# Two 1x1 maps made once, in column halves of the TensorE array, and copied three times by ScalarE

## The chip, the cores and the metric

The kernel runs on one core of one Trainium2 chip. The metric is the device time of one execution in microseconds (us). A core has a matrix engine (TensorE, PE in the profile, with its weight loads shown apart as PEld), a vector engine (VectorE, DVE), an engine for activations (ScalarE, ACT), a general engine (GpSimd, POOL) and one that here only issues transfers (SyncE, SP). Each of them works through its own instructions in order; they wait for one another by semaphores. TensorE's results land in PSUM, a small memory which DVE and ACT read; everything else lies in SBUF.

## The reference, cut to what matters

Input `x` has 8 images of 256 channels and 64x64 pixels, float32. Two layers follow each other: a block with weights made from the data (layer 0), and a block with local attention and a dynamic convolution (layer 1). Each begins with a group norm and ends with a residual sum. The change lies in the beginning of layer 0:

```python
x1 = _conv1x1(x, w1, b1)                 # 256 -> 32 channels
x2 = _conv1x1(x, w2, b2)                 # 256 -> 32 channels
x3 = _conv1x1(x, w3, b3)                 # 256 -> 256 channels
x2p = jnp.pad(x2, ((0, 0), (0, 0), (1, 1), (1, 1)), mode='reflect')
x2u = _unfold3(x2p).reshape(B, REL * K * K, H, W)   # the 9 neighbours of each pixel
h = jnp.concatenate([x1, x2u], axis=1)
h = jax.nn.relu(_bn(h, ...)); h = _conv1x1(h, cw1)
h = jax.nn.relu(_bn(h, ...)); w = _conv1x1(h, cw2, cb2)   # 9 weights per pixel and group
out = jnp.einsum('bgskhw,bgkhw->bgshw', x3u, w)     # x3u: the 9 neighbours of x3
```

So `x2` is needed at nine shifts, of which three are shifts of the column by -1, 0 and +1.

## The kernel before, in words

An image is cut into 8 bands of 8 rows, 512 pixels, so there are 64 bands. All matmuls are float32. One matmul of the program appears as two MATMUL records and two LDWEIGHTS records in the trace: the four records of `p12` in a band are two matmuls, one for each half of the 256 input channels.

**The maps (`small_maps`, L319 to L348).** For a band, TensorE makes one PSUM tile `p12` of 128 partitions by 512 pixels (L325; the trace calls it `p`). The stationary weights `w12s` hold `w2` three times and `w1` once, side by side: 32 + 32 + 32 + 32 columns. So three quarters of the output partitions carry the same map x2. ScalarE adds the bias and writes the four quarters to the SBUF tile `x2`, partitions to the same partitions: x2 shifted by one column (L332), unshifted (L332), shifted the other way (L332), and x1 (L335). Two more small activations fill the reflected border column of the two shifted copies, 8 values a partition, again from PSUM (L337, L338). Then GpSimd copies border rows from and to the neighbouring bands' tiles (L343, or L345 and L346; L348).

**What follows.** `hidden_maps` (L397) turns `x2` into `hid` on ScalarE (L406) and multiplies it on TensorE into `ph`, in four column groups of 32 (L417). `tap_weights` (L429) makes nine weights per pixel (L435), VectorE multiplies them with the neighbours of x3 (L448), GpSimd adds the products up in `xg` (L456). `value_maps` (L350) makes x3 (L357, L362).

**Scaled weights (`scaled_weights`, L288 to L317).** Once per image the group norm's scale is multiplied into `w12` and `w3` by VectorE (L296, L297), and its shift goes through the weights to the biases, by narrow matmuls (L304) and small additions (L311, L313).

**The order of the work** is written out by hand. The main loop runs over `g` from -12 to 63; for each g it makes 8 steps `s` (L971, L973). Layer 1 works on band g, layer 0 twelve bands ahead: the maps of band g + 12 are made in step 0 of g. For g below 0 only layer 0 runs (`alone`). Within a step, parts of the work are placed at fixed points by two lists, `mid` and `end`, and by `after(n, ...)`:

```python
if 0 <= g + AHEAD < B * NB:
    bq_, iq = divmod(g + AHEAD, NB)
    if s == 0:
        mid.append(lambda: small_maps(bq_, iq))
    if s == (2 if alone else 0):
        (mid if alone else end).append(lambda: value_maps(bq_, iq, 0))
```

In step 0 of a usual g, TensorE's order around the maps is: first half of the dynamic weights `pf` (L814), a transposed value tile (L595), the maps (L325), the weighted values (L736, 64-column halves of the array), second half of `pf` (L814), x3 (L357), and then the scores of step 1 (L692) and the transposed probabilities (L724). Where band g is the first of an image (i = 0), two value maps (L551) come just ahead of L325 instead of the value tile.

**PSUM tiles** of the tag `gen` are five, taken in turn: `p12` is one of them, and the fifth `gen` tile after it has to wait until ScalarE has read `p12` for the last time. On ScalarE the reads of `p12` stand behind L718 (probabilities), L597 or the value copies L560 to L569, and ahead of L819 (exponentials of `pf`), L362 (x3) and L726 (copy of the transposed probabilities). GpSimd's in-order queue has, around the maps, the sums L1010 and L825, then the border rows L343 to L348, then L842.

Of the kernel before, what the change touches and what calls it, by code (L numbers as in the profile page):

```python
# [10 lines left out]
F32 = mybir.dt.float32  # L11
BF16 = mybir.dt.bfloat16
AF = mybir.ActivationFunctionType
# [5 lines left out]
P = 128  # L19
C = 256  # L20
NCT = C // P
H = W = 64
HW = H * W
R = 8
BAND = R * W
# [5 lines left out]
REL = 32  # L31
# [41 lines left out]
PG, PB, PM, PV, PB21, PG2, PB2, PM2, PV2, PCB2 = 0, 3, 6, 9, 12, 13, 14, 15, 16, 17  # L73
# [13 lines left out]
def conv_layers_kernel(ctx: ExitStack, tc: tile.TileContext, ins: dict, out: bass.AP):  # L87
    nc = tc.nc
# [18 lines left out]
    def load(name, shape, src=None, now=True):  # L107
        t = const.tile(shape, F32, name=f"c_{name}")
        late.append(lambda: nc.scalar.dma_start(out=t, in_=ins[name] if src is None else src))
        if now:  # L110
            late.pop()()
        return t

    gmat = load("gmat", [P, P])
    par = load("par", [P, NPAR])
    chan = load("chan", [P, NCT, NCHAN], ins["chan"].rearrange("(t p) n -> p t n", p=P))
    rowp = load("rowp", [P, NROW], ins["rowp"].partition_broadcast(P))
    w12 = load("w12", [P, NCT, P], ins["w12"].rearrange("(t p) n -> p t n", p=P))
    w3 = load("w3", [P, NCT, C], ins["w3"].rearrange("(t p) n -> p t n", p=P))
    c1 = load("c1", [P, 3, REL])  # L120
    gq = load("gq", [P, P])
# [59 lines left out]
    w0 = ctx.enter_context(tc.tile_pool(name="l0", bufs=2))  # L181
    w1 = ctx.enter_context(tc.tile_pool(name="l1", bufs=2))
    ps = ctx.enter_context(tc.tile_pool(name="ps", bufs=1, space=PSUM))
# [31 lines left out]
    def after(n, f):  # L215
        later.append((place[0] + n, f))
# [71 lines left out]
    def scaled_weights(b):  # L288

        im = images[b]  # L290

        def scale(sc, bi):
            im.w12s = w0.tile([P, NCT, P], F32, tag="w12s", name=f"w12s_{b}", bufs=1)
            im.w3s = w0.tile([P, NCT, C], F32, tag="w3s", name=f"w3s_{b}", bufs=1)
            for kt in range(NCT):
                nc.vector.tensor_scalar(im.w12s[:, kt], w12[:, kt], sc[:, kt : kt + 1], None, ALU.mult)  # L296
                nc.vector.tensor_scalar(im.w3s[:, kt], w3[:, kt], sc[:, kt : kt + 1], None, ALU.mult)  # L297
            after(5, lambda: through(bi))

        def through(bi):  # L300
            pb = ps.tile([P, 1 + NCT], F32, tag="gen", name=f"pb_{b}", bufs=5)
            for m, w in enumerate((w12, w3[:, :, :P], w3[:, :, P:])):
                for kt in range(NCT):
                    nc.tensor.matmul(  # L304
                        pb[:, m : m + 1], w[:, kt], bi[:, kt : kt + 1], start=(kt == 0), stop=(kt == NCT - 1)
                    )
            after(2, lambda: biases(pb))

        def biases(pb):
            im.bias = w0.tile([P, 1 + NCT], F32, tag="bias", name=f"bias_{b}")  # L310
            nc.vector.tensor_add(im.bias[:, 0:1], pb[:, 0:1], par[:, PB21 : PB21 + 1])  # L311
            for ct in range(NCT):
                nc.vector.tensor_add(  # L313
                    im.bias[:, 1 + ct : 2 + ct], pb[:, 1 + ct : 2 + ct], chan[:, ct, CB3 : CB3 + 1]
                )

        gn_affine([im.st0[:, ct] for ct in range(NCT)], gmat, f"a{b}", scale)  # L317

    def small_maps(b, i):  # L319


        im = images[b]
        p12 = ps.tile([P, BAND], F32, tag="gen", name=f"p12_{b}_{i}", bufs=5)
        for kt in range(NCT):
            nc.tensor.matmul(p12, im.w12s[:, kt, :], im.xc[i][:, kt, :], start=(kt == 0), stop=(kt == NCT - 1))  # L325
        p12 = p12.rearrange("p (r c) -> p r c", r=R)
        t = im.x2[i] = w0.tile([P, HR, W], F32, tag="x2", name=f"x2_{b}_{i}", bufs=2)
        bias = im.bias
        for q, (dst, src) in enumerate(((1, 0), (0, 0), (0, 1))):
            n = W - (q != 1)  # L330
            s = slice(32 * q, 32 * q + 32)
            nc.scalar.activation(  # L332
                t[s, 1 : 1 + R, dst : dst + n], p12[s, :, src : src + n], AF.Identity, bias=bias[s, 0:1]
            )
        nc.scalar.activation(t[96:128, 0:R, :], p12[96:128], AF.Identity, bias=bias[96:128, 0:1])  # L335

        nc.scalar.activation(t[0:32, 1 : 1 + R, 0:1], p12[0:32, :, 1:2], AF.Identity, bias=bias[0:32, 0:1])  # L337
        nc.scalar.activation(  # L338
            t[64:96, 1 : 1 + R, W - 1 : W], p12[64:96, :, W - 2 : W - 1], AF.Identity, bias=bias[64:96, 0:1]
        )  # L340

        if i == 0:
            nc.gpsimd.tensor_copy(t[0:96, 0, :], t[0:96, 2, :])  # L343
        else:
            nc.gpsimd.tensor_copy(t[0:96, 0, :], im.x2[i - 1][0:96, R, :])  # L345
            nc.gpsimd.tensor_copy(im.x2[i - 1][0:96, R + 1, :], t[0:96, 1, :])  # L346
        if i == NB - 1:
            nc.gpsimd.tensor_copy(t[0:96, R + 1, :], t[0:96, R - 1, :])  # L348
# [507 lines left out]
    def beside(g, s):  # L856
# [52 lines left out]
# [6 lines that stand above are left out]
            if s == (3 if alone else 1):  # L915
                mid.append(lambda: value_maps(bq_, iq, 1))
# [33 lines left out]
    with tc.manual_schedule():  # L950

        for i, use in enumerate(("xc", "xc", "xr", "xr", "xs", None, None, None)):
            t = None
            if use is None:
                t = w1.tile([P, NCT, RP, W], F32, tag="yp", name=f"x_{i}", bufs=3)
                t = t.rearrange("p t r c -> p t (r c)")[:, :, :BAND]
# [14 lines left out]
        for g in range(-AHEAD, B * NB):  # L971
            b, i = divmod(g, NB)
            for s in range(STEPS):  # L973
                ct, m = divmod(s, NT // 2)
# [55 lines left out]
def _layout(inputs):  # L1030

    a = {k.replace("L0_conv_", "a_").replace("L1_conv_", "b_"): np.asarray(v) for k, v in inputs.items()}
    f = np.float32
    arr = {"x": a["x"].reshape(a["x"].shape[0], C, HW)}
    arr["w12"] = np.concatenate([a["a_w2"].T] * 3 + [a["a_w1"].T], axis=1)
    arr["w3"] = a["a_w3"].T

    def branch(v):

        o = np.zeros((P, 3) + v.shape[1:], f)  # L1040
        u = v[REL:].reshape((REL, 3, 3) + v.shape[1:])
        o[:96] = np.moveaxis(u, 2, 0).reshape((96, 3) + v.shape[1:])
        o[96:, 0] = v[:REL]
        return o

    arr["c1"] = branch(a["a_cw1"].T)

    quarter = np.tile(np.eye(REL, dtype=f) / NQR, (NQR, 1))
    arr["gq"] = np.tile(quarter, (1, NQR))
    arr["gc"] = np.repeat(quarter, SHARE, axis=1).reshape(P, NCT, P)  # L1050
    par = np.zeros((P, NPAR), f)
    for at, n in ((PG, "g"), (PB, "b"), (PM, "m"), (PV, "v")):
        par[:, at : at + 3] = branch(a[f"a_bn1_{n}"])
    par[:, PB21] = np.concatenate([a["a_b2"]] * 3 + [a["a_b1"]])
    for at, n in ((PG2, "g"), (PB2, "b"), (PM2, "m"), (PV2, "v")):
        par[:, at] = np.tile(a[f"a_bn2_{n}"], NQR)
    par[:, PCB2 : PCB2 + KK] = np.tile(a["a_cb2"].reshape(REL, KK), (NQR, 1))
    arr["par"] = par

    c2 = a["a_cw2"].reshape(REL, KK, REL).transpose(2, 1, 0)  # L1060
    arr["c2"] = np.zeros((P, KK, P), f)
    for q in range(NQR):
        arr["c2"][q * REL : (q + 1) * REL, :, q * REL : (q + 1) * REL] = c2

    chan = np.zeros((C, NCHAN), f)
    chan[:, CB3] = a["a_b3"]
    chan[:, CBQ] = a["b_bq"]
    chan[:, CBK] = a["b_bk"]
    chan[:, CBV] = a["b_bv"]
    chan[:, CBP] = np.tile(a["b_bp"], HEADS)  # L1070
    chan[:, CWP0 : CWP0 + 2] = np.tile(a["b_Wp"], (HEADS, 1))
    chan[:, CW1 : CW1 + KK] = a["b_w1"].reshape(C, KK)
    chan[:, CW2 : CW2 + KK] = a["b_w2"].reshape(C, KK)
    arr["chan"] = chan
    arr["wq"], arr["wk"], arr["wv"] = a["b_Wq"].T, a["b_Wk"].T, a["b_Wv"].T

    arr["wfc"] = a["b_Wfc"].reshape(C, KK, C)[:, [0, 1, 2, 3, 5, 6, 7, 8, 4]].transpose(2, 1, 0)

    loc = np.pad(np.linspace(-1.0, 1.0, W, dtype=f), PAD, mode="reflect")
    arr["rowp"] = np.concatenate(  # L1080
        [loc, a["b_rate1"].reshape(1), a["b_rate2"].reshape(1)]
    )

    arr["gmat"] = np.kron(np.eye(P // 8, dtype=f), np.full((8, 8), 0.125, f))
    q, k = np.arange(NQ), np.arange(NKEY)
    dr = k[None] // KW - q[:, None] // TQ
    dc = k[None] % KW - q[:, None] % TQ
    inside = (dr >= 0) & (dr < KA) & (dc >= 0) & (dc < KA)
    arr["mask"] = np.tile(np.where(inside, 0.0, NEG).astype(f), (2, 1))
    return {n: np.ascontiguousarray(v) for n, v in arr.items()}  # L1090
# [19 lines left out]
```

The softmax here doesn't subtract the row's maximum and nothing guards it: scores larger than these inputs give would overflow.

## Time and profile before

| | |
|---|---|
| three timed runs | 4334.35, 4330.35, 4332.86 us, median 4332.86 |
| span of the profiled execution | 4333.4 us |
| TensorE (PE) busy | 4174.8 us, 96% of the span |
| VectorE, ScalarE, GpSimd busy | 83%, 71%, 67% |
| maps of x1 and x2 on TensorE (L325) | 256 records, 124.5 us busy |
| copies of them on ScalarE (L332, L335, L337, L338) | 64 x (3 + 1 + 1 + 1) activations |
| granted TensorE clock | 0.992 of full speed over the span |

A row of the groups reads: line, engine, operation, what it writes and reads, shapes, count; then busy time in us and the mean duration of one in ns; then the idle time of the engine just before them, with what ended it. For TensorE a mean duration includes the way through the array and overlaps the next record; what a record costs is the distance from one start to the next, or busy time divided by count. "128*64" in a TensorE row would be 128 rows and 64 columns of the array, and "128x512" the shape of the moving operand.

### The profile page before, as it was taken

To read this page: it belongs to the slowest core of one execution; us is meant where nothing else is said; L and a number is where in the kernel's file an instruction comes from. 1 tells how busy PE (TensorE), PEld (TensorE's weight loads), DVE (VectorE), ACT (ScalarE), POOL (GpSimd) and SP (SyncE) were. 2 spreads that over 40 slices of the span, in tenths; PEclk is the share of its full clock that TensorE was granted. 3 is DMA by queue.
4 is the path that set the end of the run, shared out by engine and by line. 5 is a ranking of instruction groups with operands and counts; after the bars stand their busy time and mean duration, and the time that the engine had idled before them with its cause. 6 is when DMAs were issued, how large, how long until landed. Compare 5 with 4: busy or idle time off the path is not lost.

```text
span 4333.4 us, 72039 instructions
## 1 busy us (share of the span) xinstructions
PE 4174.8 (96%) x25004; PEld 2104.1 (49%) x25004; DVE 3577.6 (83%) x7244; ACT 3059.9 (71%) x7598; POOL 2900.3 (67%) x1778
## 2 busy tenths in 40 slices
PE   6789999999999999999999999999999999999998
PEld 3344445444454444544455444554445444454444
DVE  5778888888888888888888888888888888977777
ACT  3367777777777777877777777777677777677776
POOL 4657677676776767767776767766776777744445
PEclk9899999999999999999999999999999999999999
DMA  7754234234233333333333333343332232111100
GB/s 214 188 130 106 69 87 105 69 91 100 64 97 96 79 89 87 84 91 95 76 84 95 82 95 84 75 101 83 77 88 78 66 96 73 35 44 37 37 27 20
DMA packets 381259, 367.90 MB, mean 85 GB/s; under 512 B 55392, under 2 KB 282720, under 8 KB 380640
## 3 DMA queue, kind: packets, MB, share of 16 engines
q1 hardware_dynamic: 377568, 358.68, 32.6%
q8 instruction: 198, 3.24, 0.3%
q10 hardware_dynamic: 3328, 4.62, 0.3%
q14 instruction: 165, 1.35, 0.1%
HBM read 261.48 MB, written 101.71 MB: 84 GB/s over the span
## 4 chain that ended last, share of the span: by engine, by line
PE 61%; DVE 19%; POOL 11%; issue 5%; SPq 1%; DMA 1%; ACT 1%; POOLq 0%; ACTq 0%; DVEq 0%
PE pf L814 27%; POOL xg L456 6%; PE sco L736 5%; PE p L357 4%; PE pk L646 4%; DVE prod L448 4%; PE ptp L724 4%; PE sco L692 4%; DVE acc L771 3%; POOL ex L1010 3%; PE pq L625 3%; PE pvt L595 3%; DVE ex L832 2%; PE p L325 2%; DVE acc L797 2%
## 5 line engine op out<-in xcount | busy, mean ns | idle before, releaser
L814 PE MATMUL pf<-yp,c_wfc 128*128 128x512 f32 x4096 | 1985.1, 607 | 0.9
L456 POOL TENSOR_TENSOR xg<-xg,prod 128x1024 f32<-128x1024 f32 x549 | 1204.1, 2193 | 131.6 <-DVE prod L448 109.8
L1010 POOL TENSOR_TENSOR ex<-ex,ex 128x1024 f32<-128x1024 f32 x384 | 907.8, 2364 | 76.0 <-ACT ex L819 71.3
L814 PEld LDWEIGHTS pf<-yp,c_wfc 128*128 128x128 f32 x4096 | 696.2, 190 | 535.1 <-issue 491.0
L819 ACT ACTIVATE ex<-pf 128x512 f32<-128x512 f32 x1024 | 608.4, 594 | 453.6 <-PE pf L814 263.5
L842 POOL TENSOR_TENSOR ex<-ex,rec 128x512 f32<-128x512 f32 x128 | 163.7, 1279 | 1006.7 <-DVE rec L837 946.6
L771 DVE SCALAR_TENSOR_TENSOR acc<-yp,c_chan,acc 128x504 f32<-128x504 f32 (+3 forms) x1104 | 765.1, 693 | 55.4 <-ACT acc L762 35.0
L797 DVE SCALAR_TENSOR_TENSOR acc<-hid,c_chan,acc 128x504 f32<-128x504 f32 (+3 forms) x1024 | 758.0, 740 | 18.6 <-ACT acc L791 0.6
L448 DVE SCALAR_TENSOR_TENSOR prod<-pw,c_par,x3q 128x1040 f32<-128x1040 f32 x576 | 733.8, 1280 | 33.6 <-POOL xg L456 19.4
L718 ACT ACTIVATE prob<-prob,tot 128x196 f32<-128x196 f32 x1024 | 411.6, 451 | 427.6 <-DVE tot L716 427.6
L709 ACT ACTIVATE prob<-prob,nmax 128x196 f32<-128x196 f32 x1024 | 461.7, 455 | 85.7 <-DVE nmax L701 85.3
L736 PEld LDWEIGHTS sco<-pt,vt 112*64 112x64 f32 x8176 | 281.5, 137 | 363.5 <-issue 139.7
L701 DVE CUSTOM_DVE_ANT_0 prob<-sco,c_mask 128x196 f32<-128x196 f32 x1024 | 324.5, 355 | 159.8 <-PE sco L692 159.6
L746 DVE SCALAR_TENSOR_TENSOR xr<-sco,bv,xr 128x128 f32<-128x128 f32 x511 | 175.4, 343 | 334.5 <-PE sco L736 334.5
L736 PE MATMUL sco<-pt,vt 112*64 112x64 f32 x8176 | 350.2, 228 | 30.3 <-DVE nmax L701 28.4
L724 PE MATMUL ptp<-ident,prob 128*112 128x128 f32 x2044 | 331.6, 285 | 0.0
L726 ACT COPY pt<-ptp 112x512 f32<-112x512 f32 x511 | 296.3, 580 | 39.4 <-PE ptp L724 39.3
L692 PE MATMUL sco<-kb,qb 64*64 64x196 f32 x4096 | 294.7, 357 | 24.5 <-DVE xr L746 24.5
L724 PEld LDWEIGHTS ptp<-ident,prob 128*112 128x112 f32 x2044 | 206.4, 133 | 152.0 <-issue 66.0
L551 PE MATMUL pv<-yp,c_wv 128*128 128x512 f32 (+2 forms) x576 | 251.9, 562 | 0.0
L646 PE MATMUL pk<-yp,c_wk 128*128 128x512 f32 (+2 forms) x576 | 244.9, 552 | 0.0
L357 PE MATMUL p<-xc,w3s 128*128 128x512 f32 x512 | 243.7, 599 | 0.0
(133 smaller groups left out, 5359.2 us busy)
## 6 DMA issues: line engine op xcount, KB each, us to landing
x<-x3n SPq DMA_DIRECT2D x128, 264.0 KB, 2.1
x3q<-x SPq DMA_DIRECT2D x128, 264.0 KB, 7.1
xc<-in_x SPq DMA_DIRECT2D x64, 512.0 KB, 5.1
xg<-in_x SPq DMA_DIRECT2D x256, 128.0 KB, 4.8
x<-xg SPq DMA_DIRECT2D x256, 128.0 KB, 2.4
yp<-x SPq DMA_DIRECT2D x128, 256.0 KB, 3.3
xr<-x SPq DMA_DIRECT2D x64, 512.0 KB, 5.8
out_x<-xr SPq DMA_DIRECT2D x64, 512.0 KB, 3.1
```

The source lines that it names most:

```text
L448: nc.vector.scalar_tensor_tensor(prod[:, :, :RUN], pw[:, j, :RUN].unsqueeze(1).to_broadcast([P, SHARE, RUN]), par[:, PCB2 + k : PCB2 + k + 1],
L456: nc.gpsimd.tensor_add(im.xg[i], im.xg[i], rows(prod))
L646: nc.tensor.matmul(pk[:, :n], wk[:, kt, ct * P : (ct + 1) * P], im.yp[i][:, kt, a : a + n], start=(kt == 0), stop=(kt == NCT - 1),)
L692: nc.tensor.matmul(sco[half[t], h, :NKEY], qb[half[h], 2 * m + t].rearrange("p r c -> p (r c)"), kb[half[h], :, c0 : c0 + KW], start=True, ...
L709: nc.scalar.activation(prob[:, h, :NKEY], prob[:, h, :NKEY], AF.Exp, bias=nmax[:, h : h + 1], scale=-1.0, accum_out=tot[:, h : h + 1],)
L724: nc.tensor.transpose(ptp[:, h, ch], prob[:, h, ch * CHUNK : (ch + 1) * CHUNK], ident)
L736: nc.tensor.matmul(po[half[h], :, t * TQ : (t + 1) * TQ], im.vt[i + ch, m][:n, t, (2 * ct + h) * HD : (2 * ct + h + 1) * HD], pt[:n, h, ch ...
L771: nc.vector.scalar_tensor_tensor(o, yp[:, ct, ra + dr : rb + dr, ca + dc : cb + dc], chan[:, ct, CW1 + k : CW1 + k + 1], o, ALU.mult, ALU.add,
L797: nc.vector.scalar_tensor_tensor(o, hid[:, ra + dr : rb + dr, ca + dc : cb + dc], chan[:, ct, CW2 + k : CW2 + k + 1], o, ALU.mult, ALU.add,)
L814: nc.tensor.matmul(pf, wfc[:, kt, 2 * m + j, ct * P : (ct + 1) * P], images[b].yp[i][:, kt, PAD : PAD + R], start=(kt == 0), stop=(kt == N ...
L819: nc.scalar.activation(ex[:, j].rearrange("p (r c) -> p r c", r=R), pf, AF.Exp)
L1010: after(4, lambda ex=ex, exb=exb: nc.gpsimd.tensor_add(ex, ex, exb))
```

## The change

The weights `w12` now hold `w2` once and `w1` once: 64 columns. A band's two halves of four rows are two matmuls for each half of the input channels, one to the lower 64 output partitions and one to the upper 64, each with 256 pixels, so `p12` is 128 partitions by 256 pixels: partitions 0 to 31 hold x2 and 32 to 63 x1 of rows 0 to 3, partitions 64 to 95 and 96 to 127 the same of rows 4 to 7. ScalarE reads each half's x2 three times and its x1 once, 32 partitions at a time, and writes them to the four quarters of `x2` as before. The two border columns are copied by GpSimd, in SBUF, from the column beside, ahead of GpSimd's border rows. The bias column is made for both halves, so the narrow matmuls of the `w12` bias are four in place of two.

```diff
-    w12 = load("w12", [P, NCT, P], ...)
+    w12 = load("w12", [P, NCT, 2 * REL], ...)
...
-            im.w12s = w0.tile([P, NCT, P], F32, tag="w12s", ...)
+            im.w12s = w0.tile([P, NCT, 2 * REL], F32, tag="w12s", ...)
...
-            for m, w in enumerate((w12, w3[:, :, :P], w3[:, :, P:])):
+            for m, to, w in ((0, 0, w12), (0, 64, w12), (1, 0, w3[:, :, :P]), (2, 0, w3[:, :, P:])):
                 for kt in range(NCT):
                     nc.tensor.matmul(
-                        pb[:, m : m + 1], w[:, kt], bi[:, kt : kt + 1], start=(kt == 0), stop=(kt == NCT - 1)
+                        pb[to : to + w.shape[2], m : m + 1], w[:, kt], bi[:, kt : kt + 1],
+                        start=(kt == 0), stop=(kt == NCT - 1),
                     )
...
-        p12 = ps.tile([P, BAND], F32, tag="gen", ...)
+        p12 = ps.tile([P, R // 2, W], F32, tag="gen", ...)
         for kt in range(NCT):
-            nc.tensor.matmul(p12, im.w12s[:, kt, :], im.xc[i][:, kt, :], start=(kt == 0), stop=(kt == NCT - 1))
+            for u in range(2):
+                nc.tensor.matmul(
+                    p12[64 * u : 64 * u + 64], im.w12s[:, kt, :],
+                    im.xc[i][:, kt, u * BAND // 2 : (u + 1) * BAND // 2],
+                    start=(kt == 0), stop=(kt == NCT - 1),
+                )
...
-        for q, (dst, src) in enumerate(((1, 0), (0, 0), (0, 1))):
-            n = W - (q != 1)
-            s = slice(32 * q, 32 * q + 32)
+        for u in range(2):
+            r, o = u * R // 2, 64 * u
+            for q, (dst, src) in enumerate(((1, 0), (0, 0), (0, 1))):
+                n = W - (q != 1)
+                nc.scalar.activation(
+                    t[32 * q : 32 * q + 32, r + 1 : r + 1 + R // 2, dst : dst + n],
+                    p12[o : o + 32, :, src : src + n], AF.Identity, bias=bias[o : o + 32, 0:1],
+                )
             nc.scalar.activation(
-                t[s, 1 : 1 + R, dst : dst + n], p12[s, :, src : src + n], AF.Identity, bias=bias[s, 0:1]
-            )
-        nc.scalar.activation(t[96:128, 0:R, :], p12[96:128], AF.Identity, bias=bias[96:128, 0:1])
-
-        nc.scalar.activation(t[0:32, 1 : 1 + R, 0:1], p12[0:32, :, 1:2], AF.Identity, bias=bias[0:32, 0:1])
-        nc.scalar.activation(
-            t[64:96, 1 : 1 + R, W - 1 : W], p12[64:96, :, W - 2 : W - 1], AF.Identity, bias=bias[64:96, 0:1]
-        )
+                t[96:128, r : r + R // 2, :], p12[o + 32 : o + 64], AF.Identity, bias=bias[o + 32 : o + 64, 0:1]
+            )
+
+        nc.gpsimd.tensor_copy(t[0:32, 1 : 1 + R, 0:1], t[0:32, 1 : 1 + R, 2:3])
+        nc.gpsimd.tensor_copy(t[64:96, 1 : 1 + R, W - 1 : W], t[64:96, 1 : 1 + R, W - 3 : W - 2])
```

The inputs `w12` and the bias column of `par` are laid out to match on the host, outside the timed program.

More of the change, by code (lines that the diff above doesn't have):

```diff
@@ L117, in conv_layers_kernel @@
     rowp = load("rowp", [P, NROW], ins["rowp"].partition_broadcast(P))
-    w12 = load("w12", [P, NCT, P], ins["w12"].rearrange("(t p) n -> p t n", p=P))
+    w12 = load("w12", [P, NCT, 2 * REL], ins["w12"].rearrange("(t p) n -> p t n", p=P))
     w3 = load("w3", [P, NCT, C], ins["w3"].rearrange("(t p) n -> p t n", p=P))
@@ L292, in scale @@
         def scale(sc, bi):
-            im.w12s = w0.tile([P, NCT, P], F32, tag="w12s", name=f"w12s_{b}", bufs=1)
+            im.w12s = w0.tile([P, NCT, 2 * REL], F32, tag="w12s", name=f"w12s_{b}", bufs=1)
             im.w3s = w0.tile([P, NCT, C], F32, tag="w3s", name=f"w3s_{b}", bufs=1)
@@ L322, in small_maps @@
         im = images[b]
-        p12 = ps.tile([P, BAND], F32, tag="gen", name=f"p12_{b}_{i}", bufs=5)
+        p12 = ps.tile([P, R // 2, W], F32, tag="gen", name=f"p12_{b}_{i}", bufs=5)
         for kt in range(NCT):
-            nc.tensor.matmul(p12, im.w12s[:, kt, :], im.xc[i][:, kt, :], start=(kt == 0), stop=(kt == NCT - 1))
-        p12 = p12.rearrange("p (r c) -> p r c", r=R)
+            for u in range(2):
[4 more added lines that the diff above has]
+                )
         t = im.x2[i] = w0.tile([P, HR, W], F32, tag="x2", name=f"x2_{b}_{i}", bufs=2)
         bias = im.bias
-        for q, (dst, src) in enumerate(((1, 0), (0, 0), (0, 1))):
-            n = W - (q != 1)
-            s = slice(32 * q, 32 * q + 32)
+        for u in range(2):
[6 more added lines that the diff above has]
+                )
             nc.scalar.activation(
-                t[s, 1 : 1 + R, dst : dst + n], p12[s, :, src : src + n], AF.Identity, bias=bias[s, 0:1]
+                t[96:128, r : r + R // 2, :], p12[o + 32 : o + 64], AF.Identity, bias=bias[o + 32 : o + 64, 0:1]
             )
-        nc.scalar.activation(t[96:128, 0:R, :], p12[96:128], AF.Identity, bias=bias[96:128, 0:1])
-        nc.scalar.activation(t[0:32, 1 : 1 + R, 0:1], p12[0:32, :, 1:2], AF.Identity, bias=bias[0:32, 0:1])
-        nc.scalar.activation(
-            t[64:96, 1 : 1 + R, W - 1 : W], p12[64:96, :, W - 2 : W - 1], AF.Identity, bias=bias[64:96, 0:1]
-        )
+        nc.gpsimd.tensor_copy(t[0:32, 1 : 1 + R, 0:1], t[0:32, 1 : 1 + R, 2:3])
+        nc.gpsimd.tensor_copy(t[64:96, 1 : 1 + R, W - 1 : W], t[64:96, 1 : 1 + R, W - 3 : W - 2])
         if i == 0:
@@ L1034, in _layout @@
     arr = {"x": a["x"].reshape(a["x"].shape[0], C, HW)}
-    arr["w12"] = np.concatenate([a["a_w2"].T] * 3 + [a["a_w1"].T], axis=1)
+    arr["w12"] = np.concatenate([a["a_w2"].T, a["a_w1"].T], axis=1)
     arr["w3"] = a["a_w3"].T
@@ L1053, in _layout @@
         par[:, at : at + 3] = branch(a[f"a_bn1_{n}"])
-    par[:, PB21] = np.concatenate([a["a_b2"]] * 3 + [a["a_b1"]])
+    par[:, PB21] = np.concatenate([a["a_b2"], a["a_b1"]] * 2)
     for at, n in ((PG2, "g"), (PB2, "b"), (PM2, "m"), (PV2, "v")):
```

## The prediction

> **What bounds the kernel now.** I first read busy time by stage, to see which engine is full and where.
>
> ```profile
> core 0: us, PE busy (x) PEld busy (x) DVE busy (x) ACT busy (x) POOL busy (x), PEclk, DMA share, GB/s
> 0.00:265.00 265.00, 189.85 (x794) 96.83 (x795) 179.22 (x243) 99.83 (x181) 149.84 (x104) 0.90 0.74 202
> 265.00:1845.00 1580.00, 1550.32 (x9379) 783.49 (x9377) 1340.75 (x2717) 1159.85 (x2884) 1104.13 (x670) 1.00 0.35 86
> 1845.00:3600.00 1755.00, 1721.92 (x10463) 870.51 (x10463) 1490.45 (x3011) 1281.61 (x3178) 1245.51 (x754) 1.00 0.34 85
> ```
>
> Until 265 us only layer 0 runs and no engine is full. From there to 3600 us TensorE is busy 98% of the time, VectorE 85%, ScalarE 73%, GpSimd 71%. Of the 64 bands' maps, 13 start before 265 us and 51 in the full stage.
>
> Next, the chain of work that ended last, for one band of the full stage, to see whether the maps are on it.
>
> ```profile
> 1050.86 0.44 PE pvt L595 x4
> 1051.29 1.72 PE p L325 x4
> 1053.01 0.62 PE sco L736 x16
> 1053.63 1.91 PE pf L814 x4
> ...
> 1077.77 0.64 PE sco L736 x16
> 1078.40 0.02 issue
> 1078.43 0.35 DVE xr L746
> ```
>
> The maps stand on the chain with their full 1.72 us. The chain leaves TensorE only at 1078.4 us, for VectorE and GpSimd, and VectorE's work there was itself released by TensorE: by the gap list VectorE had idled 2.48 us before that L746. So the whole later part moves when TensorE moves. "PE p L325 2%" on the page (some 87 us) says the same of all: 51 x 1.72 = 88.
>
> Third, the timeline of TensorE, for what a record costs from start to start, with full and with split columns.
>
> ```profile
> 1006.56 1.88 PE L814 MATMUL pf<-yp,c_wfc 128*128 128x512 f32 x4
> 1008.38 0.65 PE L417 MATMUL ph<-hid,c_c 128*32 128x128 f32 x16
> 1008.95 1.98 PE L646 MATMUL pk<-yp,c_wk 128*128 128x512 f32 x4
> ...
> 1051.13 1.88 PE L325 MATMUL p<-xc,w12s 128*128 128x512 f32 x4
> 1052.94 0.69 PE L736 MATMUL sco<-pt,vt 112*64 112x64 f32 x16
> 1053.56 0.70 PE L814 MATMUL pf<-yp,c_wfc 128*128 128x512 f32 x1
> ```
>
> A full-width record of 512 pixels takes 1.72 / 4 = 0.43 us, or 0.84 ns a pixel. Sixteen records of L417, 128 pixels each, would take 1.72 us in turn and take 0.57: its four groups of 32 columns run beside each other. Sixteen of L736, 64 pixels in two groups of 64 columns, would take 0.86 and take 0.62; in pairs they would take 0.43, and the rest is fixed cost. The step from L325 to L736 is 1.81 in place of 1.72, so going from full columns to split ones costs 0.09; going back costs as much (estimate: the last pair of L736 lies 0.15 before L814, and a pair lasts 0.06).
>
> **What the Trainium skill says.** "TensorEngine Tiling (Array Packing)", Key Properties: column tiles work independently, and a change of tiling mode drains the engine. The trace agrees with both, as just read. "ScalarE: Activation LUTs", Rules for kernel authors, budgets about 0.3 us an activation and 0.83 ns an element; the trace's own pair, 267 ns for 8 and 671 for 504 elements, gives 0.26 us and 0.81 ns, and I use that. "SBUF — State Buffer", SBUF: two separate sides: VectorE's fast modes and GpSimd hold a shared port by turns, for a whole instruction. The trace agrees: L832 takes 0.42 us at 1058.40 us while GpSimd idles, and 2.39 in the chain at 1090.83.
>
> **The change, part by part.**
>
> *TensorE, full stage.* Removed: 4 records of 512 pixels and the 0.09 of going to split columns for L736, 1.81 us. Added: 8 records of 256 pixels in two column groups, that is 4 pairs of 256 x 0.84 = 0.215, so 0.86; 0.09 to enter split columns after L595; 0.05 for the first pair, whose next weights aren't loaded yet (L736's first pair starts 0.107 before its second, the others 0.058). L736 follows in the same 64-column halves, so nothing on leaving. Sum 1.00, a gain of 0.80 us a band. The trace has no split record longer than 196 pixels, so the overlap of two long ones is inferred: from no overlap (1.86, a loss of 0.05 and more) to no fixed cost (0.86, a gain of 0.95); I take 0.80.
>
> *ScalarE.* Removed: 3 x 0.68 + 0.68 + 2 x 0.27 = 3.3 us a band, start to start. Added: eight of 252 or 256 elements, 0.47 each by the pair above, with gaps 3.85. So +0.5 a band. No row shows an activation from one group of partitions to another. The bounds are 0.40 (half of 0.68 plus little, so no more than now) and 0.68 each (no gain from halving, +2.1 a band); I take 0.47. Behind these reads wait L819, L362 and L726, and TensorE, for the PSUM tile:
>
> ```profile
> 1838.27 0.27 ACT L338 ACTIVATE x<-p,bias 32x8 f32<-32x8 f32 x1
> 1838.56 0.60 ACT L819 ACTIVATE ex<-pf 128x512 f32<-128x512 f32 x1
> ...
> 1839.45 1.88 PE L814 MATMUL pf<-yp,c_wfc 128*128 128x512 f32 x4
> ```
>
> This is step 0 to 1 of an image's first band. The fifth PSUM tile after the maps' is that L814's: ScalarE released it at 1838.53, 0.9 us ahead. With TensorE 0.8 earlier and ScalarE 0.5 later, L814 waits 0.4. ScalarE doesn't start sooner, because it begins these reads 1.4 us after TensorE has finished, behind L560 to L569. So these 6 bands gain 0.4. In the other 45 the fifth tile after is taken 3.0 us or more after release: 3.0 − 0.8 − 0.5 leaves 1.7. There the half microsecond is hidden further on: L726 comes 0.3 later, ScalarE then idles 0.31 before L819 and 1.32 before L718, which waits for VectorE.
>
> *GpSimd.* Two copies of 32 x 8 values: the nearest is the border row, 234 ns for 96x64; bounds 0.1 and 0.5 (single strided values may be slow), taken 0.2. They wait for ScalarE's last write, as L343 and L346 already do (2.6 us a band on the mean), so that queue gets 0.5 + 0.4 us longer there. L345, which ran without this wait, now stands behind it, and is needed only in the next band. Queued behind are L842, after 9.3 us of idle, and in an image's seventh band L621, whose keys are used three steps later. Cost 0. The copies may meet L832, moved to 1057.6: held up to 0.5, against VectorE's idle 0.84 before the L746 at 1062.88. Cost 0.
>
> *Per image* (six in the full stage). L304 has 16 records for 12, at 0.105 each (1.26 us for 12 to L435), and enters and leaves split columns: 4 x 0.07 + 0.18, +0.45. The scaling L296 halves, but its 0.66 and 1.06 are mostly waits for GpSimd's port: −0.15. Sum +0.3.
>
> *Start.* The first maps run at half clock and are on the chain with 3.62 us: gain 1.5, less 0.5 for L304. Three more on the chain gain 0.6 each (both mode changes are paid). The other nine run beside transfers and VectorE: 0. Sum −2.8. In the maps at 264 us ScalarE is late (it starts 3.0 after TensorE), and I count 0.
>
> *Sum.* 45 x 0.80 = 36.0; 6 x 0.40 = 2.4; start 2.8; less 6 x 0.3 = 1.8: 39.4 us. The profiled span, 4333.4, is within a microsecond of the timed median, 4332.86. 4333.4 − 39.4 = **4294 us**.
>
> **The rivals.**
>
> *ScalarE takes half back.* If an activation of half the size costs 0.68, ScalarE has +2.1 us. L718 then comes about 0.8 late in its step, VectorE's queue with it; half of that, 0.4, reaches TensorE in 45 bands (18 us), and the 6 first bands gain nothing (2.4): 4314. For it: fixed parts are large here. Against: the two small activations took 267 ns.
>
> *Hidden anyway.* VectorE and GpSimd hold the chain from 1078 to 1101 us in this band; were their state carried over from band to band, the gain would end in waits of L692 and L736, now 0.7 us a band: 4325 to 4333. Against: VectorE's 2.48 us of idle at 1078.43.
>
> *More than forecast.* No drain and no fixed cost: 0.95 x 45 + 0.55 x 6 + 3 = 49: 4284.
>
> *Slower.* The halves of long records don't overlap, for each streams its own 256 pixels. Then a band has 8 x 0.215 + 0.14 = 1.86 on TensorE for 1.81, and ScalarE's 0.5 in the first bands: 51 x 0.05 + 6 x 0.5 + 1.8 + 2 = 9 us: 4342. It decides from the point where a pair takes over 0.42 us. Against: L417's four groups stream four different pieces and overlap. This is also the case in which the change doesn't do what it says.
>
> **How the numbers follow.** Forecast (4288 to 4301) 0.66; half taken back (4302 to 4318) 0.16; more (4278 to 4287) 0.08; hidden anyway 0.06; slower 0.04. The range 4283 to 4313 holds the forecast, most of the second and half of the third, about 0.82. A measurement of this kernel tells about 0.2%, 8.7 us, from no change. Faster: the first three and a little of the fourth, 0.91; same 0.06; slower 0.03.
>
> **What would show it.** Records of L325: 512, 128*64, 256 pixels; from L325's start to L736's about 0.9 us where it was 1.81 (the rest lies ahead of it). ScalarE's eight near 0.47. A new wait of L814 for ScalarE, 0.4 us, in first bands alone. Usual bands 63.5 us apart where they were 64.3. GpSimd's L842 still after idle time. The forecast is wrong if the pairs start one after the other, or if waits of TensorE (L692 and L736 for VectorE) grow by over 10 us in all.

## The result, and the profile after

The changed kernel takes 4297.91 us (median of four, 4294.2 to 4301.8), the kernel before 4333.6 in the same runs (4330.35 to 4335.14): ratio 0.9919, 95% interval 0.9902 to 0.9936. A second set of runs gave 4297.45 us and 0.9917 (0.9902 to 0.9932). The profiled span is 4300.0 us, 33.4 less than before.

Line numbers have moved: L325 is L328 now, L736 is L744, L814 is L822, L357 is L365; in the experiments they differ by a few again. Busy time by stage; the full stage begins and ends at the same bands as before, the cut between its two lines lies some 12 us earlier in its band:

```profile
core 0: us, PE busy (x) PEld busy (x) DVE busy (x) ACT busy (x) POOL busy (x), PEclk, DMA share, GB/s
260.00:1820.00 1560.00, 1527.69 (x9434) 779.15 (x9432) 1334.13 (x2706) 1157.75 (x2907) 1113.40 (x717) 0.99 0.35 88
1820.00:3567.00 1747.00, 1712.79 (x10648) 873.36 (x10644) 1495.94 (x3024) 1300.32 (x3263) 1256.37 (x809) 1.00 0.34 86
```

TensorE is as full as before, 98%, in a stage of 3307 us for 3335; no other engine has taken its place. In the first line the granted clock is 0.99 where it was 1.00, which will matter. The chain of work that ended last, for the band shown of before:

```profile
1042.85 0.44 PE pvt L603 x4
1043.29 1.01 PE p L328 x8
1044.30 0.47 PE sco L744 x16
1044.77 1.91 PE pf L822 x4
...
1068.90 0.64 PE sco L744 x16
1069.54 0.02 issue
1069.57 0.35 DVE xr L754
```

The maps have 1.01 us of it where they had 1.72, and L744 behind them 0.47 where it had 0.62. The way from the value tile to the first VectorE link was 27.57 us (1050.86 to 1078.43) and is 26.72 now: 0.85 less. Nothing on it waits, and it is again TensorE that releases VectorE. TensorE's timeline gives the same from start to start:

```profile
1042.69 0.60 PE L603 MATMUL pvt<-ident,vc 128*112 128x128 f32 x4
1043.22 1.08 PE L328 MATMUL p<-xc,w12s 128*64 128x256 f32 x8
1044.13 0.64 PE L744 MATMUL sco<-pt,vt 112*64 112x64 f32 x16
1044.70 1.55 PE L822 MATMUL pf<-yp,c_wfc 128*128 128x512 f32 x3
```

From L328 to L744 it takes 0.91 us where it took 1.81. Eight records of 256 pixels in turn would take 1.72, so the two halves of the columns do run beside each other. From L744 to L822 it takes 0.57 where it took 0.62. The groups by form give the new operations (the last number before the idle time is the mean in ns):

```profile
L339 ACT ACTIVATE x<-p,bias 32x252 f32<-32x252 f32 x256 | 118.1, 461 | 45.6 <-PE p L328 38.3 <-DMA c_wk<-in_wk 5.0
L343 ACT ACTIVATE x<-p,bias 32x256 f32<-32x256 f32 x128 | 59.7, 466 | 2.4
L348 POOL COPY x<-x 32x8 f32<-32x8 f32 x64 | 12.3, 191 | 48.3 <-ACT x L339 47.9
L347 POOL COPY x<-x 32x8 f32<-32x8 f32 x64 | 12.0, 188 | 138.0 <-ACT x L339 138.0
```

In the first band of an image, TensorE now has a wait that it didn't have. ScalarE's timeline, then TensorE's, and last two of TensorE's lines before:

```profile
1825.93 0.47 ACT L343 ACTIVATE x<-p,bias 32x256 f32<-32x256 f32 x1
```

```profile
1825.46 0.65 PE L732 MATMUL ptp<-ident,prob 128*112 128x128 f32 x4
1826.45 1.98 PE L822 MATMUL pf<-yp,c_wfc 128*128 128x512 f32 x4 [0.34 <-ACT x L343]
1828.27 0.59 PE L633 MATMUL pq<-yp,c_wq 128*128 128x512 f32 x1
```

```profile
1838.96 0.65 PE L724 MATMUL ptp<-ident,prob 128*112 128x128 f32 x4
1841.16 1.88 PE L625 MATMUL pq<-yp,c_wq 128*128 128x512 f32 x4
```

L822 starts 0.05 us after ScalarE's last read of the maps has ended at 1826.40: it takes the fifth PSUM tile after `p12`. From L732 to L822 it takes 0.99 us where it took 0.49 (1838.96 to 1839.45), so TensorE loses 0.50; the list of waits counts 0.34 of it, and 2.0 us in six times over the whole execution. L822 itself then takes 1.82 us to the next start where it took 1.71.

**The distance of the bands**, from one start of the maps to the next, compared band by band with before, says where the 33.4 us come from. A first band is one in which layer 1 begins an image (i = 0); all others are called usual. Undisturbed usual bands are 0.86 us closer, the six first bands 0.21 to 0.27. Between the first and the last of the 51 bands of the full stage lie 50 such distances, 44 usual and 6 first ones: 44 x 0.86 + 6 x 0.24 = 39.3 us. Two distances stand out the other way: one longer by 3.8 in place of shorter by 0.86, one by 0.6. In both the TensorE clock was granted at half: 10.2 us at 1538 and 3.4 at 504. They cost 4.7 and 1.5. One more usual distance, without half clock, is only 0.58 shorter, which costs 0.3 (see `acts_alone`). 39.3 less 6.5 is 32.8; measured over these bands: 32.9. The start gave 0.6, the end lost 0.1.

The view by windows of the first of these two places:

```profile
1534.70:1538.10 3.40, 1.64 (x19) 1.06 (x19) 3.37 (x8) 1.47 (x5) 0.88 (x1) 1.00 0.01 2
1538.10:1548.30 10.20, 10.20 (x41) 6.17 (x40) 9.38 (x19) 5.20 (x15) 4.70 (x4) 0.50 0.00 1
```

Ahead of it TensorE had been busy for 1.64 of 3.4 us, because L744 waited 1.76 us for VectorE in the fourth band of the image (for L709, which reads the scores and writes `nmax`); then came 10.2 us at half clock. The wait is in the profile before as well, in all six fourth bands, there without a loss of clock.

### The profile page after: what moved, and what is told of

It is laid out like the page before. It is cut to its first block, busy times and chain, and to the rows that moved or that the text cites. A ratio compares the mean times of both kernels' runs of the same rounds, so it can differ in the third digit from the quotient of the medians.

```text
span 4300.0 us, 72936 instructions
## 1 busy us (share of the span) xinstructions
PE 4137.6 (96%) x25292; PEld 2097.9 (49%) x25292; DVE 3575.0 (83%) x7244; ACT 3080.2 (72%) x7726; POOL 2924.9 (68%) x1906
## 4 chain that ended last, share of the span: by engine, by line
PE 59%; DVE 19%; POOL 12%; issue 5%; ACT 3%; SPq 1%; DMA 1%; POOLq 0%; ACTq 0%; DVEq 0%
PE pf L822 27%; POOL xg L464 6%; PE sco L744 5%; PE pk L654 4%; PE p L365 4%; PE ptp L732 4%; DVE prod L456 4%; PE sco L700 4%; DVE acc L779 3%; POOL ex L1018 3%; PE pq L633 3%; PE pvt L603 2%; DVE ex L840 2%; DVE acc L805 2%; DVE rec L841 2%
## 5 line engine op out<-in xcount | busy, mean ns | idle before, releaser
L822 PE MATMUL pf<-yp,c_wfc 128*128 128x512 f32 x4096 | 1989.4, 608 | 2.9 <-ACT x L343 2.0
L822 PEld LDWEIGHTS pf<-yp,c_wfc 128*128 128x128 f32 x4096 | 697.3, 190 | 538.4 <-issue 492.0
L850 POOL TENSOR_TENSOR ex<-ex,rec 128x512 f32<-128x512 f32 x128 | 163.5, 1277 | 939.8 <-DVE rec L845 879.6
L744 PEld LDWEIGHTS sco<-pt,vt 112*64 112x64 f32 x8176 | 286.1, 137 | 331.7 <-issue 110.7
L709 DVE CUSTOM_DVE_ANT_0 prob<-sco,c_mask 128x196 f32<-128x196 f32 x1024 | 324.5, 355 | 144.6 <-PE sco L700 144.3
L744 PE MATMUL sco<-pt,vt 112*64 112x64 f32 x8176 | 347.7, 227 | 29.8 <-DVE nmax L709 27.9
L732 PE MATMUL ptp<-ident,prob 128*112 128x128 f32 x2044 | 332.8, 286 | 0.0
L700 PE MATMUL sco<-kb,qb 64*64 64x196 f32 x4096 | 295.2, 358 | 24.9 <-DVE xr L754 24.7
L732 PEld LDWEIGHTS ptp<-ident,prob 128*112 128x112 f32 x2044 | 207.2, 134 | 152.6 <-issue 75.7
L365 PE MATMUL p<-xc,w3s 128*128 128x512 f32 x512 | 244.0, 600 | 0.0
```

Of the source, the lines that this page charges most:

```text
L700: nc.tensor.matmul(sco[half[t], h, :NKEY], qb[half[h], 2 * m + t].rearrange("p r c -> p (r c)"), kb[half[h], :, c0 : c0 + KW], start=True, ...
L732: nc.tensor.transpose(ptp[:, h, ch], prob[:, h, ch * CHUNK : (ch + 1) * CHUNK], ident)
L744: nc.tensor.matmul(po[half[h], :, t * TQ : (t + 1) * TQ], im.vt[i + ch, m][:n, t, (2 * ct + h) * HD : (2 * ct + h + 1) * HD], pt[:n, h, ch ...
L822: nc.tensor.matmul(pf, wfc[:, kt, 2 * m + j, ct * P : (ct + 1) * P], images[b].yp[i][:, kt, PAD : PAD + R], start=(kt == 0), stop=(kt == N ...
```

## The experiments

All ratios are to the kernel before in the same runs.

**again: the changed kernel once more.** Are the stretches at half clock the change's?

> The changed kernel once more. In its first profile the usual bands of the full stage are 0.86 us closer together than before and the first bands of an image 0.24, which makes 45 x 0.86 + 6 x 0.24 = 40 us; the span is only 33.4 us shorter, and three stretches with half the TensorE clock (6.8 us at 265, 3.4 at 504, 10.2 at 1538 us) lie in it that the profile before doesn't have at these places. Theory, chance: the band distances repeat to 0.02 us, while the half-clock stretches after 280 us lie elsewhere or are missing, and the times spread over some 8 us from 4292 to 4302. Rival, the change itself brings these stretches: they stand at the same places again, and all times are near 4300.

4297.45 us (4295.94 to 4299.28), ratio 0.9917. Usual bands 0.86 closer, first bands 0.26 to 0.30. One long stretch, 10.2 us, now at 2052 us: again an image's fourth band, but another image's. The places aren't fixed; so far the theory is right. In the nine profiles in which VectorE scales the weights in that band (both kernels compared and all experiments but the last), with six such bands each, 10 of 54 were followed by half clock. One was in `acts_alone`, whose TensorE work is that of before. So it also comes without the change, and not in every execution. Whether the change makes it likelier stays open. The mean granted clock of the timed executions hints at it: 0.989 to 0.991 in the eight of the changed kernel, 0.991 to 0.994 in the 22 of the kernel before that ran beside the experiments and in the twelve of `acts_alone`. But this mean takes in the start, where every profile has stretches at half clock, and one of 10.2 us lowers it by 0.0012 only.

**acts_alone: ScalarE's and GpSimd's part without TensorE's.** On the kernel before:

```diff
-        for q, (dst, src) in enumerate(((1, 0), (0, 0), (0, 1))):
...
-        nc.scalar.activation(t[96:128, 0:R, :], p12[96:128], ...)
...
+        for u in range(2):
+            r = u * R // 2
+            for q, (dst, src) in enumerate(((1, 0), (0, 0), (0, 1))):
+                n = W - (q != 1)
+                s = slice(32 * q, 32 * q + 32)
+                nc.scalar.activation(
+                    t[s, r + 1 : r + 1 + R // 2, dst : dst + n], p12[s, r : r + R // 2, src : src + n], ...)
+            nc.scalar.activation(t[96:128, r : r + R // 2, :], p12[96:128, r : r + R // 2], ...)
+        nc.gpsimd.tensor_copy(t[0:32, 1 : 1 + R, 0:1], t[0:32, 1 : 1 + R, 2:3])
+        nc.gpsimd.tensor_copy(t[64:96, 1 : 1 + R, W - 1 : W], t[64:96, 1 : 1 + R, W - 3 : W - 2])
```

> The kernel before, with TensorE's maps as they were (128 columns, 512 pixels), but with the eight half-height activations and the two border columns on GpSimd. Theory, the whole gain is TensorE's: ScalarE has 0.5 us more a band, GpSimd 0.9, the fifth PSUM tile in first bands had 0.91 us in hand, so nothing waits: 4334 us, within 3 of before, and TensorE's waits for ScalarE at L814 are none. Rival, the new activations or copies cost or win something by themselves (ScalarE's order, GpSimd's port): 4338 or more, or 4328 or less.

4336.88 us (twelve runs, 4331.57 to 4340.12), ratio 1.0006 (0.9998 to 1.0015). Usual bands differ from before by 0.005 us at the median, first ones by 0.01 to 0.04; `pf` has no wait for ScalarE. Two distances stand out: one is 4.7 longer, with 10.2 us at half clock in it, and one 0.27, where TensorE at 1161 us waits 1.18 us for VectorE in place of 0.91; the changed kernel loses the same 0.3 in that band, in both profiles. Otherwise the new activations and copies neither cost nor win anything by themselves. What else the change touches, the scaling of the weights and the bias matmuls, comes once per image, and the bands with it gain what others gain. So the gain is that of TensorE's maps.

**halves_in_turn: does the overlap need the halves in alternation?** On the changed kernel:

```diff
-        for kt in range(NCT):
-            for u in range(2):
+        for u in range(2):
+            for kt in range(NCT):
                 nc.tensor.matmul(
```

> The changed kernel with the two loops of the maps' matmuls exchanged: both matmuls of the lower half of the columns, then both of the upper half. Theory, records start in the order they are issued and one overlaps only with a neighbour of the other half: the lower half's four records take 0.86 us, the upper half's can start only with the last of them, so L328 to L744 takes 0.64 us more (1.55 for 0.91), the usual bands lose that: 45 x 0.64 = 29, about 4326 us. Rival, each half of the columns has a queue of its own: 0.91 us and 4297 us, as the changed kernel.

A miss, and the rival is right:

```profile
458.74 1.09 PE L328 MATMUL p<-xc,w12s 128*64 128x256 f32 x8
459.65 0.46 PE L744 MATMUL sco<-pt,vt 112*64 112x64 f32 x9
```

From L328 to L744 it takes 0.91 us, as in alternation, though four records of one half are issued ahead of the first of the other. In the single records behind this view the second starts 13 ns after the first (458.741 and 458.754), in the changed kernel 7. The trace doesn't say to which half a record belongs. But the offset has changed with the order, and eight records take little more than four in turn would (4 x 0.215 = 0.86), so two of them run at a time from the first on. Work for one half of the columns doesn't hold up what is queued behind it for the other. The time is 4303.47 us (ratio 0.9926, 0.9912 to 0.9941); usual bands are at 0.85 all the same, and its profile has half clock behind three images' fourth bands, two long and one short, which is 2 x 4.7 + 1.5 = 11 us.

**pool_shifts: ScalarE's queue made short.** On the changed kernel; ScalarE has four activations a band in place of eight:

```diff
-            for q, (dst, src) in enumerate(((1, 0), (0, 0), (0, 1))):
...
+            nc.scalar.activation(t[32:64, r + 1 : r + 1 + R // 2, :], p12[o : o + 32], ...)
             nc.scalar.activation(t[96:128, r : r + R // 2, :], p12[o + 32 : o + 64], ...)
+        nc.gpsimd.tensor_copy(t[0:32, 1 : 1 + R, 1:W], t[32:64, 1 : 1 + R, 0 : W - 1])
+        nc.gpsimd.tensor_copy(t[64:96, 1 : 1 + R, 0 : W - 1], t[32:64, 1 : 1 + R, 1:W])
```

> The changed kernel with ScalarE writing only the unshifted x2 and x1 (four activations a band, 1.9 us for 3.8), and GpSimd making the two shifted copies in SBUF (32 x 8 x 63 each). Theory, ScalarE costs only in the six first bands, where L822 waits for the PSUM tile: its wait is gone, these bands come 0.86 closer than before and not 0.24, 3.7 us less than the changed kernel, 4294; usual bands stay at 0.86. Rival one, ScalarE's longer queue also costs in usual bands: they gain over 0.9, and the time falls below 4285. Rival two, GpSimd's longer queue or its port costs VectorE: 4300 or more.

4289.76 us, ratio 0.9902 (0.9885 to 0.9918). In the first bands, where the changed kernel waited:

```profile
1815.67 0.65 PE L731 MATMUL ptp<-ident,prob 128*112 128x128 f32 x4
1816.16 1.88 PE L821 MATMUL pf<-yp,c_wfc 128*128 128x512 f32 x4
```

The wait is gone, and the first bands are 0.85 to 0.90 closer than before; usual ones stay at 0.86. That is the theory: 6 x 0.6 = 3.7 us. GpSimd's copies took 0.59 and 0.60 us and cost the bands nothing. The median fell by 7.7 us below `again` and not by 3.7. In the two profiles the clock makes the difference: between the first and the last of the 51 bands this kernel takes 8.5 us less than `again`, 3.5 of them in the first bands and 4.7 in the one band that has half clock in `again`; neither this profile nor the next has any behind the waits for `nmax`. The mean clocks of the timed executions go the same way, 0.990 in each of `again` and 0.991 or 0.992 here. Where in them it was lost, no profile shows.

**pool_shifts_again: the same once more.**

> The kernel of pool_shifts once more, for a tighter interval and a second profile. Usual and first bands 0.86 closer than before, as there; half-clock stretches after 280 us only behind the TensorE wait of 1.8 us in an image's fourth band, in some of the six images, and 3.8 us lost with each long one: 4286 to 4294 us.

4286.08 us, ratio 0.9895 (0.9878 to 0.9911), the same band distances but for one usual one that is 1.35 shorter, and no half clock in its profile between 270 us and the end of the maps.

**acts_for_columns: ScalarE's queue made long.** On the changed kernel, the border columns from PSUM again, in four activations of four values:

```diff
-        nc.gpsimd.tensor_copy(t[0:32, 1 : 1 + R, 0:1], t[0:32, 1 : 1 + R, 2:3])
-        nc.gpsimd.tensor_copy(t[64:96, 1 : 1 + R, W - 1 : W], t[64:96, 1 : 1 + R, W - 3 : W - 2])
+        for u in range(2):
+            r, o = u * R // 2, 64 * u
+            for q, to, at in ((0, 0, 1), (2, W - 1, W - 2)):
+                nc.scalar.activation(
+                    t[32 * q : 32 * q + 32, r + 1 : r + 1 + R // 2, to : to + 1],
+                    p12[o : o + 32, :, at : at + 1], AF.Identity, bias=bias[o : o + 32, 0:1],
+                )
```

> The changed kernel with the border columns made by ScalarE again, from PSUM: four more activations of 4 values a band (0.27 each, 1.07 us), two GpSimd copies less. Theory, ScalarE's time counts only where the PSUM tile is late: first bands lose 1.07 each, 6.4 us in all, and are some 0.8 us further apart than before; usual bands, with 1.65 us in hand, stay at 0.86: about 4304. Rival, ScalarE's time also counts in usual bands: they are 0.4 or more further apart, and the time is 4315 or more.

4302.87 us (two runs), ratio 0.9932. The first bands are 0.77 to 0.81 us further apart than before, usual ones stay at 0.86. TensorE's waits (total, times, longest) have

```profile
PE pf L827 <- ACT x L350: 8.4, 6, 1.4
```

for 2.0 in the changed kernel. A microsecond of ScalarE in each of 64 bands is paid in six of them.

**half_channels: is TensorE still what bounds?** On the changed kernel, the maps over half of the input channels:

```diff
-        for kt in range(NCT):
+        for kt in range(1):
...
-                    start=(kt == 0), stop=(kt == NCT - 1),
+                    start=True, stop=True,
```

> The changed kernel without the second half of the input channels in the maps of x1 and x2 (the matmuls of kt = 1 are left out, so x1 and x2 are wrong by that half): TensorE has another 0.43 us less in each band, everything else is as it is. Theory, in usual bands TensorE still sets the end and the band's other engines follow it: usual bands 0.86 + 0.43 = 1.29 us closer than before, first bands as in the changed kernel (0.25), because L822 waits for ScalarE, which doesn't start earlier: 20 us less, about 4278. Rival, the gain of the change has used up the slack of VectorE and GpSimd: usual bands stay near 0.86, and waits of L700 and L744 for VectorE grow.

4278.02 us (two runs), ratio 0.9875. Two successive usual bands in TensorE's timeline:

```profile
392.16 0.65 PE L328 MATMUL p<-xc,w12s 128*64 128x256 f32 x4
...
455.14 0.65 PE L328 MATMUL p<-xc,w12s 128*64 128x256 f32 x4
```

They are 62.98 us apart, before 64.26 (397.65 to 461.91): 1.28 less, of 0.86 + 0.43 = 1.29 expected; over all usual bands 1.26 to 1.34, but for one of 1.02 and three with 3.4 us of half clock, again in fourth bands. First bands are at 0.27 to 0.31, held by ScalarE as in the changed kernel. TensorE's waits for VectorE haven't grown: 27.9 us at L744, as in the changed kernel, and 24.6 for 24.7 at L700. VectorE and GpSimd follow another 0.43 us a band: their slack isn't used up.

**pool_shifts_act_scales: the wait behind the half clock.** On `pool_shifts`:

```diff
-                nc.vector.tensor_scalar(im.w12s[:, kt], w12[:, kt], sc[:, kt : kt + 1], None, ALU.mult)
-                nc.vector.tensor_scalar(im.w3s[:, kt], w3[:, kt], sc[:, kt : kt + 1], None, ALU.mult)
+                nc.scalar.activation(im.w12s[:, kt], w12[:, kt], AF.Copy, scale=sc[:, kt : kt + 1])
+                nc.scalar.activation(im.w3s[:, kt], w3[:, kt], AF.Copy, scale=sc[:, kt : kt + 1])
```

> pool_shifts, and the scaling of the weights (L296, L297) on ScalarE in place of VectorE, where it takes 4.1 us an image, most of it waiting while GpSimd works. Theory, TensorE's wait of 1.8 us for nmax in those six bands comes from these four operations, and the half-clock stretches at these places come from that wait: both are gone, 6 x 1.8 = 10.8 us less and no half-clock stretch between 280 us and the end of the maps at 3560; about 4278 us, with ScalarE some 1.6 us longer in these bands, hidden. Rival, the wait stays because VectorE is late there for other reasons, or moves to L822 or L733 behind ScalarE: 4287 to 4290, as pool_shifts.

4277.13 us (4275.49 to 4279.09), ratio 0.9873 (0.9858 to 0.9887): some 9 us below `pool_shifts_again` in the same set of runs, and below both kernels compared here. TensorE's waits for `nmax` in `pool_shifts_again`, and then in this kernel:

```profile
PE sco L743 <- DVE nmax L708: 28.2, 62, 1.8
```

```profile
PE sco L743 <- DVE nmax L708: 17.3, 55, 0.6
```

10.9 us less, and the longest falls from 1.8 to 0.6. The six bands concerned are 2.82 us closer than before where usual ones are 0.86. The first half of the theory is shown. No half clock follows in these bands either. But elsewhere it followed only 10 of 54 waits, and in `pool_shifts` and `pool_shifts_again` none of twelve, so that could be luck in six: the second half isn't shown.

## Why the prediction was right

*TensorE bounds the full stage, and what comes later moves with it.* Right. `half_channels` shows it beyond the change itself, `acts_alone` that nothing else gains. The rival in which VectorE and GpSimd hide the gain is out.

*0.80 us a band.* It is 0.86. The stage from L595 to L736 gained 0.81 as worked out (1.92, which is 0.11 + 1.81, to 0.20 + 0.91). The 0.05 more came behind it: L744's first pair follows L328 in the same halves of the columns now and starts 0.060 us before its second, where it was 0.106, so that L744 has 0.57 to L822 for 0.62. I had counted that fixed cost for L328, and not that it leaves L744. (That it is a wait for weights, as the prediction has it, no run here shows.)

*ScalarE 0.47 an activation and 3.85 in all.* 0.46 and 0.47, and 3.83 (1822.57 to 1826.40). Reading one group of partitions and writing another costs nothing extra: in `acts_alone`, which writes to the partitions that it reads, they take 0.46 and 0.47 too.

*First bands gain 0.4.* They gain 0.24. The mechanism, the place (L814, now L822) and the releaser are the forecast's. The term was mis-sized: from the start of the maps to L732 TensorE gains 0.93 us. Of that, the wait takes 0.50 and not 0.40, the L822 behind it another 0.10, which I hadn't counted, and entering split columns ahead of the next band's maps 0.09. That leaves 0.24.

*GpSimd's copies 0.2, cost 0; per image +0.3.* The copies take 0.19. The per-image term was too high: at full clock the sixteen records of L304 take 1.25 us, as the twelve had with 1.26, and the bands with it gain 0.87 to 0.91, no less than others. (The sum had charged 0.07 for each of the four more, after reading 0.105 for each of the twelve.) *Start 2.8:* not to be told. The start of the first of the 51 bands moved by −0.6 in one profile of the changed kernel and −1.3 in the other, and by −5.5 in `acts_alone`, where TensorE's maps are as before.

*Sum 39.4.* The 50 band distances alone give 39.3 without the stretches at half clock. That these agree is luck: for the same distances the forecast has 44 x 0.80 + 6 x 0.40 − 6 x 0.3 = 35.8, and the rest is its start and one more usual band. Usual bands and the per-image term gave more than forecast, first bands less, the start 2.2 less in the first profile. The stretches at half clock weren't in the forecast, and take 6 us in the first profile, 5 in the second; the medians are 35.7 and 36.7 below before.

*The slower case* needed pairs of over 0.42 us; a pair takes 0.215 (four in 0.86, with 0.05 of first load 0.91). *Half taken back by ScalarE* is out: an activation takes 0.46 and not 0.68 us, and in `acts_for_columns`, where ScalarE is busy with the maps for 4.7 us a band in place of 3.2, usual bands lose nothing.

*The other signs.* TensorE's waits for VectorE didn't grow: 24.5 us at L692 and 28.4 at L736 before, 24.7 and 27.9 after. GpSimd's L842, now L850, still starts after idle time, 940 us of it in all for 1007. Usual bands are 63.4 us apart where they were 64.3.

## What to carry to other kernels

Where a stationary operand repeats itself to fill the columns of the array, leave the copies out and give each half of the columns its own half of the pixels; the engine that empties PSUM can make the copies, if it has time. Put such a matmul beside others of the same split: here the 0.09 us of going to split columns only moved from L736 to the maps (0.11 to 0.20 ahead of them), and L744 became 0.05 shorter. Before adding work to an engine with slack, count how long its queue holds each PSUM tile, and how far behind the tile is taken again: the half microsecond here was free in 45 bands and paid in six, and where it would be paid could be read ahead of time.

## What was not expected of the hardware

The two halves of the columns don't need alternating work: with four records of one half queued first, a second record still started 13 ns after the first, and all eight took 0.91 us. And a single TensorE wait of 1.8 us was in 10 of 54 cases followed by 3.4 or 10.2 us at half clock, which cost 1.5 or 4.7 us where the distances of the bands were measured. Two of them cost 6.2 us in the first profile, nearly the spread of 4294 to 4302 us between executions of the changed kernel, though only the profiled ones can be looked into. Why some of these waits are followed by it and most are not stays open.
